# Second-layer weight preparation moved within the image cycle, in larger pieces and in place, and the S1 product split seven to two

## The chip, the cores and the metric

The kernel runs on one core of one Trainium2 chip. The metric is the device time of one execution in microseconds, as the median of several runs. A profiled execution is recorded beside them, with the instructions of each engine: PE (TensorE matmul) with its weight loads (PEld), DVE (VectorE), ACT (ScalarE), POOL (GpSimd) and SP (SyncE, which only issues DMAs here).

## What is computed

Sixteen images of 256 channels, 28 by 28, pass through a group norm, two "table lookup" convolutions with batch norm, a squeeze-and-excite gate and residual additions, in float32. Each 3x3 convolution is done per channel c by a soft choice among 16 centroids of the 9-element patch:

```python
d = jnp.sum(p * p, axis=-1)[..., None] - 2.0 * jnp.einsum('bncs,cks->bnck', p, centroids) + jnp.sum(centroids * centroids, axis=-1)[None, None]
attn = jax.nn.softmax(-d, axis=-1)
lut = jnp.einsum('cks,cso->cko', centroids, w_sub)
out = jnp.einsum('bnck,cko->bno', attn, lut)
...
out = amm_conv3x3(out1, centroids1, wsub1)
out = relu(bn_inference(out, ...1))
out = amm_conv3x3(out, centroids2, wsub2)
out = bn_inference(out, ...2)
out = se_layer(out, se_w1, se_b1, se_w2, se_b2)
return x + relu(out + gn(x))
```

The kernel multiplies the softmax weights with the centroids first (logits, exponentials, numerators "na" for taps 0 to 7, "nb" for tap 8 and the denominators), divides, and multiplies the resulting 9 stacks "q" of 128 rows by w_sub.

## The kernel before

All 16 images go through layer 1, then all through layer 2. An image is four blocks, (channel half hh, row half t) in the order of BLOCKS, and a block is two steps; so an image takes eight steps, n*8 to n*8 + 7, and the products of an image trail its logits by five to twelve steps. Nothing is scheduled by a tool: `at(step, sub, function, ...)` puts a job into a list, and the list, sorted by step and then by the fraction `sub`, is the order in which each engine gets its instructions. Each engine takes its own in order. Below, the remainder of a step is its number modulo 8.

In every step PE does 16 logit matmuls (sub 0.1), the denominators "nb" or the numerators "na" of an earlier block (1.0), 16 more logit matmuls (1.1) and one product of 9 stacks (2.0). ACT takes the exponentials of the logits out of PSUM; DVE takes reciprocals, spreads them (`spread`) and scales the numerators into the q buffers (`scale_a`); POOL scales what ACT copied (`scale_q`, 1.3).

The products use seven multiplications in place of eight (L43): A11, S1, S3, S2, S4, A12, A22, with the q buffers of two blocks subtracted from each other on POOL (`mix`, L523) between them. Product S1 is cut in two: KO[:8], eight stacks, in step 6 of an image, and KO[8:], one stack, in step 7. KO puts the pairs of stacks in the order 2 to 7, 8, 0, 1, and POOL makes the mixed buffers in the same order, pair (0, 1) last, at (step 5, 2.5). PSUM is a ring of four double banks with a fixed role per step.

Patch tiles `pt` are two, each loaded by six DMAs of SP at sub 1.5, two steps before the logits that read them. The loads wait until the second logits of their own step have released the tile. The patches come from DRAM copies home1 (layer 1) and home2 (layer 2). In layer 1, POOL scatters an image's result, channel-sorted by a rank found in the first images, from hpad into home2 with four indirect DMAs (`to_home2`, L590) at remainders 4 to 6: both halves of channel block 0, then those of block 1. The next image's group norm, its home1 write (`to_home1`, remainder 4) and the load of the image after (remainder 6) stand in the same list.

While layer 1 runs, the tables of layer 2 are made from the unsorted weights. This preparation is what the change moves:

- h0: image 0's result, kept in DRAM until the rank is known, is loaded and scattered (`h0_load`, `h0_put`).
- codes: centroids2 in two layouts, scattered by rank into d_sk and d_ks.
- sub: wsub2, in three pieces per channel half (4 and 4 stacks and 1), scattered into d_wa and d_wb.
- wd: the distance table, gathered from d_sk with nine DMAs (`prep_wd0`), spread on DVE (`prep_wd1`), squared on POOL and centred with three matmuls (`prep_wd2`, `prep_wd3`), centred by its mean and stored to d_wd[1] (`prep_wd4`).
- cw: the numerator tables, gathered from d_ks with eight DMAs, made on DVE (cwa) and POOL (cwb, four parts), stored to d_cwa and d_cwb.
- sums: the combined weights S1 to S4, two stacks at a time: four loads, four POOL additions or subtractions, four stores.

All of it goes through one staging tile of 128 x 1568 (`stage`, tag "pb", one buffer), so each load waits until the tile's former readers, stores and scatters included, are done. In layer 2 the same buffer holds the wide path's z.

Of the kernel before, what the change touches and what calls it, by code (L numbers as in the profile page):

```python
# [43 lines left out]
    (5, "A11", 0, KO), (6, "S1", 0, KO[:8]), (7, "S1", 0, KO[8:]), (8, "S3", 1, KO), (9, "S2", 0, KO),  # L44
# [29 lines left out]
def kernel(  # L74
# [628 lines left out]
    def sub_load(o, part):  # L703
        n = 4 * C if part < 2 else C
        nc.sync.dma_start(stage()[:, :n], wsub2[o * P : (o + 1) * P, part * 4 * C : part * 4 * C + n])

    def sub_put(o, part):
        n = 4 * C if part < 2 else C
        scatter(d_wa if part < 2 else d_wb, 2 + part, o, pw["st"][:, :n])

    def prep_wd0():
        st = stage()
        nc.gpsimd.memset(st[:, :512], 0.0)
# [21 lines left out]
    def prep_wd4():  # L735
        st = pw.pop("st")
# [3 lines left out]
        nc.sync.dma_start(d_wd[1], st[:, 512:1536])  # L740
# [17 lines left out]
    def prep_cwb(part):  # L758
# [7 lines left out]
        if part == 3:  # L766
            pw.pop("st")
            nc.sync.dma_start(d_cwb, st[:, 512:1536])

    def sums_load(k0):  # L770
        st = stage()
        n = min(2, NS - k0)
        for hh in range(2):
            for o in range(2):
                at0 = 256 * (2 * hh + o)
                if n == 2:
                    nc.sync.dma_start(
                        st[:, at0 : at0 + 256].rearrange("p (s n) -> p s n", n=P),
                        view(d_wa, (hh * 8 + k0) * P * C + o * P, [[C, P], [P * C, 2], [1, P]]),
                    )  # L780
                else:
                    nc.sync.dma_start(st[:, at0 : at0 + P], d_wb[hh * P : hh * P + P, o * P : (o + 1) * P])

    def sums_put(k0):
        st = pw.pop("st")
        n = min(2, NS - k0)
        f = {w: st[:, 256 * i : 256 * i + P * n] for i, w in enumerate(("A11", "A21", "A12", "A22", "S1"))}
        for dst, a, b, op in (
            ("S1", "A21", "A22", ALU.add), ("A21", "A11", "A21", ALU.subtract),
            ("A22", "S1", "A11", ALU.subtract), ("A12", "A12", "A22", ALU.subtract),  # L790
        ):
            nc.gpsimd.tensor_tensor(f[dst], f[a], f[b], op)
        for n0, w in (("S1", "S1"), ("S3", "A21"), ("S2", "A22"), ("S4", "A12")):
            nc.sync.dma_start(d_ws[n0][:, k0 : k0 + n, :], f[w].rearrange("p (s n) -> p s n", n=P))
# [256 lines left out]
    at(49, 0.6, prep_wd0)  # L1051
    at(50, 0.3, prep_wd1)
    for part in range(3):
        at(51 + 2 * part, 0.02, prep_wd2, part)
        at(51 + 2 * part, 2.1, prep_wd3, part, 51 + 2 * part)
    at(59, 1.9, prep_wd4)
    at(60, 0.6, prep_cw0)
    at(61, 1.9, prep_cwa)
    for part in range(4):
        at((67, 68, 75, 76)[part], 2.3, prep_cwb, part)  # L1060
    at(92, 2.3, load_se)
    for n in range(5):
        at(82 + 8 * n, 0.6, sums_load, 2 * n)
# [198 lines left out]
```

## Time and profile before

| | us |
|---|---|
| median of 3 runs | 2680.17 |
| lowest and highest run | 2678.79, 2683.46 |
| profiled execution | 2684.49 |
| its span, first to last instruction | 2683.0 |
| PE busy in it | 2613.8 |
| longest stretches off PE in the chain of waits | 244.01 to 260.51, 492.00 to 507.90 |

The mean granted clock of PE over the span is 0.993. The page lists busy times of each engine; the chain of waits follows the work that ended last back from the end, and lists its pieces by start and length; the windows view sums each engine's busy time between chosen bounds. In the trace every fp32 matmul shows as two records, and one stack of a product takes 0.65 us on PE. An image is best measured from the start of one of its products to the same product of the next image; in the prediction that is the product at remainder 0. Step 24 starts its product at 282.68, step 128 at 1348.24, and step 16 at 190.39.

### The profile page before, as it was taken

What the parts mean: (1) busy time and instruction counts of PE and PEld (TensorE: products, weight loads), DVE (VectorE), ACT (ScalarE), POOL (GpSimd) and SP (SyncE); (2) the same over time, 40 slices, a digit from 0 to 9 for tenths busy, and PEclk for the clock granted to TensorE, in tenths of its full rate; (3) what the DMA queues carried; (4) which work ended last, traced back from release to release, by engine and by line L of the source; (5) the groups of instructions that cost most, each with busy time, mean ns of one, the idle gap of its engine ahead of it and who ended that gap; (6) DMA issues with size and microseconds to landing.
All of it is one profiled execution on the core that took longest, in us unless ns stands there. A gap on an engine that the chain in (4) does not pass through costs nothing.

```text
span 2683.0 us, 85705 instructions
## 1 busy us (share of the span) xinstructions
PE 2613.8 (97%) x36984; PEld 1261.1 (47%) x36984; DVE 1773.8 (66%) x3786; ACT 1354.7 (50%) x1873; POOL 1903.7 (71%) x1334
## 2 busy tenths in 40 slices
PE   4999999999999999999999999999999999999997
PEld 1344444444444444444444444444444444444444
DVE  4785666667666556656577767677767677767675
ACT  2443444444445444444455555555555655555653
POOL 3755677666776666766578687788787788787786
PEclk8999999999999999999999999999999999999999
DMA  8665667755666666666584555545555555555551
GB/s 180 162 158 147 155 159 201 195 139 138 158 165 168 178 156 145 164 176 158 127 191 108 111 127 123 116 111 109 122 127 123 116 113 108 121 127 123 116 114 51
DMA packets 223337, 374.39 MB, mean 140 GB/s; under 512 B 30360, under 2 KB 193736, under 8 KB 222952
## 3 DMA queue, kind: packets, MB, share of 16 engines
q1 hardware_dynamic: 216008, 334.87, 54.0%
q0 software_dynamic: 6944, 33.95, 3.5%
q8 instruction: 295, 4.83, 0.8%
q14 instruction: 90, 0.74, 0.1%
HBM read 288.93 MB, written 79.80 MB: 137 GB/s over the span
## 4 chain that ended last, share of the span: by engine, by line
PE 86%; DMA 1%; POOL 1%; issue 1%; DVE 1%; ACT 0%; SPq 0%; POOLq 0%; DVEq 0%; ACTq 0%
PE acc L518 46%; PE lg L384 15%; PE na L434 12%; PE nb L448 12%; DMA home<-hpad,col 1%; POOL qp L527 1%; PE sep L814 0%; ACT e L395 0%; DMA pt<-home 0%; PE sep L803 0%; DVE qp L510 0%; DVE rb L491 0%; POOL home L590 0%; POOL qo L525 0%; PE sqp L288 0%
## 5 line engine op out<-in xcount | busy, mean ns | idle before, releaser
L395 ACT ACTIVATE e<-lg 128x784 f32<-128x784 f32 x960 | 738.8, 821 | 720.2 <-PE lg L384 714.9
L527 POOL TENSOR_TENSOR qp<-qp,qp 128x784 f32<-128x784 f32 x512 | 944.6, 1870 | 163.5 <-DVE qp L510 163.0
L518 PE MATMUL acc<-qp,w_S 128*128 128x392 f32 x2048 | 743.2, 503 | 7.7 <-POOL qp L527 6.3
L491 DVE STREAM_SHUFFLE rb<-r 128x392 f32<-128x392 f32 x1024 | 550.6, 604 | 0.0
L518 PE MATMUL acc<-qp,w_A 128*128 128x392 f32 x1536 | 546.5, 499 | 0.1
L518 PEld LDWEIGHTS acc<-qp,w_S 128*128 128x128 f32 x2048 | 376.1, 190 | 356.6 <-POOL qp L527 39.1
L384 PE MATMUL lg<-pt,wd 32*32 32x392 f32 x16384 | 500.6, 504 | 27.0 <-DMA pt<-home 16.3
L518 PEld LDWEIGHTS acc<-qp,w_A 128*128 128x128 f32 x1536 | 284.1, 190 | 247.9 <-DVE qp L510 37.6
L510 DVE TENSOR_TENSOR qp<-na,rb 128x784 f32<-128x784 f32 x352 | 334.1, 972 | 98.1 <-PE na L434 84.9
L462 DVE SCALAR_TENSOR_TENSOR r<-nb,kst,r 128x392 f32<-128x392 f32 x128 | 79.9, 624 | 464.5 <-ACT r L458 464.5
L448 PE MATMUL nb<-e,cwb 64*32 64x392 f32 x8192 | 382.4, 497 | 2.1 <-issue 1.0
L434 PE MATMUL na<-e,cwa 64*32 64x392 f32 x8192 | 377.5, 494 | 0.1
L476 DVE RECIPROCAL r<-r 128x392 f32<-128x392 f32 x128 | 333.2, 2603 | 4.4
L499 POOL TENSOR_TENSOR qp<-qp,rb 128x784 f32<-128x784 f32 x160 | 297.4, 1871 | 2.4
L448 PEld LDWEIGHTS nb<-e,cwb 64*32 64x32 f32 x8192 | 181.4, 107 | 195.8 <-issue 57.1
L384 PEld LDWEIGHTS lg<-pt,wd 32*32 32x32 f32 x16384 | 127.5, 103 | 309.0 <-issue 261.6
L499 POOL TENSOR_TENSOR qo<-qo,rb 128x392 f32<-128x392 f32 x128 | 132.0, 1031 | 197.7 <-DVE rb L487 197.5
L434 PEld LDWEIGHTS na<-e,cwa 64*32 64x32 f32 x8192 | 182.5, 106 | 186.8 <-issue 78.0
L590 POOL DMA_INDIRECT home<-hpad,col x60 | 60.6, 1011 | 185.9 <-DMA home<-hpad,col 91.2
L458 ACT ACTIVATE r<-nb,kst 128x392 f32<-128x392 f32 x128 | 86.8, 678 | 177.4 <-PE nb L448 177.4
L419 POOL TENSOR_TENSOR z<-z,mx 128x1568 f32<-128x1568 f32 x32 | 92.1, 2879 | 86.4 <-DVE mx L413 86.4
L504 ACT COPY qp<-na 128x784 f32<-128x784 f32 x160 | 130.1, 813 | 26.0 <-PE na L434 24.0
(154 smaller groups left out, 1744.5 us busy)
## 6 DMA issues: line engine op xcount, KB each, us to landing
pt<-home SPq DMA_DIRECT2D x768, 209.0 KB
pt<-home SPq DMA_DIRECT2D x756, 104.5 KB
home<-xpad SPq DMA_DIRECT2D x31, 899.0 KB
xt<-in_x SPq DMA_DIRECT2D x30, 784.0 KB
out_dram<-y SPq DMA_DIRECT2D x32, 392.0 KB
w_S<-d_wS SPq DMA_DIRECT2D x4, 576.0 KB
st<-in_wsub SPq DMA_DIRECT2D x4, 512.0 KB
st<-d_wa SPq DMA_DIRECT2D x16, 128.0 KB
```

The costliest lines, as they stand in the source:

```text
L384: nc.tensor.matmul(bk[32 * c : 32 * c + 32, :N].rearrange("p (r w) -> p r w", w=W), lhsT=wts["wd", u["hh"]][32 * i : 32 * i + 32, mm, c, : ...
L395: nc.scalar.activation(eg[:, 2 * i : 2 * i + 2, :], bk[:, :, :N], AF.Exp, scale=2.0)
L419: nc.gpsimd.tensor_tensor(zk, zk, mx.unsqueeze(2).to_broadcast([P, N // 4, K]), ALU.subtract)
L434: nc.tensor.matmul(bs[32 * i : 32 * i + 32, r, :N], lhsT=wts["cwa", u["hh"]][64 * r : 64 * r + 64, mm, i, :], rhs=es[64 * r : 64 * r + 64, ...
L448: nc.tensor.matmul(bs[32 * i : 32 * i + 32, r, :N], lhsT=wts["cwb", u["hh"]][64 * r : 64 * r + 64, mm, i, :], rhs=es[64 * r : 64 * r + 64, ...
L476: nc.vector.reciprocal(u["r"], u["r"])
L491: nc.vector.stream_shuffle(rb[:, r, :], u["r"], mask_of(2 * mm + r))
L499: nc.gpsimd.tensor_tensor(q, q, u.pop(("rb", mm)), ALU.mult)
L504: nc.scalar.copy(pair(u, mm), u.pop(("na", mm))[:, :, :N])
L510: nc.vector.tensor_mul(pair(u, mm), u.pop(("na", mm))[:, :, :N], rb)
L518: nc.tensor.matmul(accs[key][:, :N], lhsT=wl[w][:, k, :], rhs=us["q", k], start=first and n == 0, stop=last and n == len(ks) - 1,)
L527: nc.gpsimd.tensor_tensor(pair(out_u, mm), pair(in0, mm), pair(in1, mm), ALU.subtract)
```

## The change

The steps and sub-positions of most preparation jobs are changed. wsub2 is loaded in two pieces per channel half in place of three (the ninth stack comes with the second). The clearing of the wd staging tile, the stores of wd and cwb, and the arithmetic and the stores of the sums become jobs of their own (`prep_clear`, `prep_keep`, `sums_make`, `sums_put`). The sums are made three stacks at a time, and S1 and S2 are written over A22 and A11, so that four tiles suffice in place of five. Product S1 is cut 7 to 2.

```diff
-    (5, "A11", 0, KO), (6, "S1", 0, KO[:8]), (7, "S1", 0, KO[8:]), (8, "S3", 1, KO), (9, "S2", 0, KO),
+    (5, "A11", 0, KO), (6, "S1", 0, KO[:7]), (7, "S1", 0, KO[7:]), (8, "S3", 1, KO), (9, "S2", 0, KO),
...
     def sub_load(o, part):
-        n = 4 * C if part < 2 else C
+        n = (4 + part) * C
         nc.sync.dma_start(stage()[:, :n], wsub2[o * P : (o + 1) * P, part * 4 * C : part * 4 * C + n])
     def sub_put(o, part):
-        n = 4 * C if part < 2 else C
-        scatter(d_wa if part < 2 else d_wb, 2 + part, o, pw["st"][:, :n])
+        scatter(d_wa, 2 + part, o, pw["st"][:, : 4 * C])
+        if part == 1:
+            scatter(d_wb, 4, o, pw["st"][:, 4 * C : 5 * C])
+    def prep_clear():
+        nc.gpsimd.memset(stage()[:, :512], 0.0)
     def prep_wd0():
-        st = stage()
-        nc.gpsimd.memset(st[:, :512], 0.0)
+        st = pw["st"]
...
     def prep_wd4():
-        st = pw.pop("st")
+        st = pw["st"]
...
-        nc.sync.dma_start(d_wd[1], st[:, 512:1536])
+    def prep_keep(dst):
+        nc.sync.dma_start(dst, pw.pop("st")[:, 512:1536])
...
-        if part == 3:
-            pw.pop("st")
-            nc.sync.dma_start(d_cwb, st[:, 512:1536])
+    def sums_of():
+        return {w: pw["st"][:, 3 * P * i : 3 * P * i + 3 * P] for i, w in enumerate(("A11", "A21", "A12", "A22"))}
     def sums_load(k0):
...
+        n = min(3, NS - 1 - k0)
+        for w, t in sums_of().items():
+            hh, o = {"A11": (0, 0), "A21": (0, 1), "A12": (1, 0), "A22": (1, 1)}[w]
+            nc.sync.dma_start(
+                t[:, : n * P].rearrange("p (s n) -> p s n", n=P),
+                view(d_wa, (hh * 8 + k0) * P * C + o * P, [[C, P], [P * C, n], [1, P]]),
+            )
+            if n < 3:
+                nc.sync.dma_start(t[:, n * P :], d_wb[hh * P : hh * P + P, o * P : (o + 1) * P])
+    def sums_make():
+        f = sums_of()
         for dst, a, b, op in (
-            ("S1", "A21", "A22", ALU.add), ("A21", "A11", "A21", ALU.subtract),
-            ("A22", "S1", "A11", ALU.subtract), ("A12", "A12", "A22", ALU.subtract),
+            ("A22", "A21", "A22", ALU.add), ("A21", "A11", "A21", ALU.subtract),
+            ("A11", "A22", "A11", ALU.subtract), ("A12", "A12", "A11", ALU.subtract),
         ):
             nc.gpsimd.tensor_tensor(f[dst], f[a], f[b], op)
+    def sums_put(k0):
+        f = sums_of()
+        pw.pop("st")
+        for n0, w in (("S1", "A22"), ("S3", "A21"), ("S2", "A11"), ("S4", "A12")):
+            nc.sync.dma_start(d_ws[n0][:, k0 : k0 + 3, :], f[w].rearrange("p (s n) -> p s n", n=P))
...
-        at(20 + 3 * o, 0.6, h0_load, o)
+        at(24 + 2 * o, 0.6 + 2 * o, h0_load, o)
         for r in range(2):
-            at(*(((21, 1.77), (22, 2.95)), ((24, 2.95), (25, 1.78)))[o][r], h0_put, o, r)
-        at(32 + 2 * o, 0.6, codes_load, o)
+            at(25 + 2 * o + r, 0.2 if r else 1.9, h0_put, o, r)
+        at(32 + 2 * o, 2.6, codes_load, o)
         for i in range(2):
-            at(33 + 2 * o, 1.78 if o == i == 0 else 1.805, codes_put, o, i)
-        for part in range(3):
-            c = 36 + 6 * o + 2 * part
-            at(c, 0.6, sub_load, o, part)
-            at(c + 1, (1.77, 2.7, 1.78, 1.805)[(3 * o + part) % 4 if o == 0 else (3, 0, 1)[part]], sub_put, o, part)
-    at(49, 0.6, prep_wd0)
-    at(50, 0.3, prep_wd1)
+            at(33 + 2 * o, 1.9, codes_put, o, i)
+        for part in range(2):
+            c = 40 + 8 * o + 2 * part
+            at(c, 2.6, sub_load, o, part)
+            at(c + 1, 1.9, sub_put, o, part)
+    at(56, 1.95, prep_clear)
+    at(57, 1.6, prep_wd0)
+    at(60, 0.3, prep_wd1)
     for part in range(3):
-        at(51 + 2 * part, 0.02, prep_wd2, part)
-        at(51 + 2 * part, 2.1, prep_wd3, part, 51 + 2 * part)
-    at(59, 1.9, prep_wd4)
-    at(60, 0.6, prep_cw0)
-    at(61, 1.9, prep_cwa)
+        c = (65, 67, 73)[part]
+        at(c, 0.02, prep_wd2, part)
+        at(c, 2.1, prep_wd3, part, c)
+    at(75, 1.9, prep_wd4)
+    at(75, 2.7, prep_keep, d_wd[1])
+    at(80, 2.6, prep_cw0)
+    at(83, 1.9, prep_cwa)
     for part in range(4):
-        at((67, 68, 75, 76)[part], 2.3, prep_cwb, part)
+        at((83, 84, 89, 91)[part], (2.3, 0.9, 1.9, 1.9)[part], prep_cwb, part)
+    at(91, 2.7, prep_keep, d_cwb)
     at(92, 2.3, load_se)
-    for n in range(5):
-        at(82 + 8 * n, 0.6, sums_load, 2 * n)
-        at(83 + 8 * n, 2.3, sums_put, 2 * n)
+    for n in range(3):
+        at(96 + 8 * n, 2.6, sums_load, 3 * n)
+        at(97 + 8 * n, 1.9, sums_make)
+        at(98 + 8 * n, 2.6, sums_put, 3 * n)
```

More of the change, by code (lines that the diff above doesn't have):

```diff
@@ L765, in prep_cwb @@
             nc.gpsimd.tensor_add(f[:, m], f[:, m], ones_b[:, m % 4, :].unsqueeze(1).to_broadcast([P, 4, 32]))
-        if part == 3:
-            pw.pop("st")
-            nc.sync.dma_start(d_cwb, st[:, 512:1536])
+    def sums_of():
+        return {w: pw["st"][:, 3 * P * i : 3 * P * i + 3 * P] for i, w in enumerate(("A11", "A21", "A12", "A22"))}
     def sums_load(k0):
[L771 to L787, printed above, removed]
+        stage()
+        n = min(3, NS - 1 - k0)
[7 more added lines that the diff above has]
+                nc.sync.dma_start(t[:, n * P :], d_wb[hh * P : hh * P + P, o * P : (o + 1) * P])
```

2 lines of the change are left out of this document (removed).

## The prediction

> **What bounds the kernel now.** I read the page first, then the chain of waits in order of time, and then the windows view, cut at the first product of an image. One row of the page says who sets the time:
>
> ```profile
> PE 2613.8 (97%) x36984; PEld 1261.1 (47%) x36984; DVE 1773.8 (66%) x3786; ACT 1354.7 (50%) x1873; POOL 1903.7 (71%) x1334
> ```
>
> The work of PE itself is not changed, so only stretches in which PE waits, or runs slowly around a wait, can be won. The windows view gives their size (columns: bounds, length, busy time of PE, PEld, DVE, ACT, POOL, granted clock, DMA share, GB/s):
>
> ```profile
> 190.39:239.25 48.86, 46.56 (x589) 22.83 (x589) 30.06 (x72) 17.72 (x24) 35.32 (x36) 0.97 0.45 95
> 239.25:282.68 43.43, 40.95 (x569) 18.28 (x567) 25.42 (x59) 20.04 (x28) 25.18 (x25) 0.96 0.78 218
> 282.68:614.37 331.69, 326.92 (x4623) 157.89 (x4623) 208.25 (x482) 152.05 (x208) 224.01 (x170) 1.00 0.66 169
> 614.37:859.33 244.96, 243.33 (x3464) 117.80 (x3463) 159.67 (x364) 114.23 (x156) 166.90 (x140) 1.00 0.63 157
> 859.33:1187.82 328.49, 326.26 (x4618) 158.60 (x4617) 204.09 (x477) 152.20 (x208) 220.95 (x171) 1.00 0.65 164
> 1187.82:1230.91 43.09, 43.09 (x590) 21.75 (x589) 25.58 (x62) 17.62 (x24) 28.89 (x25) 1.00 0.49 103
> 1230.91:1268.10 37.19, 37.19 (x568) 17.85 (x567) 23.17 (x53) 20.41 (x28) 22.39 (x16) 1.00 0.74 200
> 1348.24:1430.01 81.77, 80.91 (x1152) 38.31 (x1151) 56.53 (x112) 40.88 (x54) 59.58 (x39) 1.00 0.76 179
> 2314.30:2394.71 80.41, 80.41 (x1158) 39.02 (x1157) 56.71 (x113) 46.68 (x66) 63.02 (x39) 1.00 0.53 118
> ```
>
> Rows six and seven are one image of layer 1 with next to no preparation: 43.09 + 37.19 = 80.28 us. An image of layer 2 takes 80.41 with PE busy throughout, so there is nothing to win in layer 2 behind its first image. Against 80.28 an image, steps 24 to 56 lose 331.69 - 321.12 = 10.57, steps 56 to 80 lose 4.12, steps 80 to 112 lose 7.37: 22.06 us. Image 2 loses 48.86 - 43.09 = 5.77 in its first half and 43.43 - 37.19 = 6.24 in its second. The first image of layer 2 loses 81.77 - 80.41 = 1.36. This is the pot.
>
> The chain shows where the loss starts:
>
> ```profile
> 244.01 8.51 issue
> 252.53 7.98 DMA home<-hpad,col
> ...
> 445.80 6.12 PE acc L518 x18
> 456.51 6.12 PE acc L518 x18
> 467.34 6.12 PE acc L518 x18
> 478.06 6.12 PE acc L518 x18
> 492.00 7.94 DMA home<-hpad,col
> 500.20 7.70 DMA home<-hpad,col
> 529.03 6.12 PE acc L518 x18
> ```
>
> It leaves PE at the scatter of an image into home2, in steps with remainder 4 to 6. POOL issues the second half of a channel block only when the first has landed, and ScalarE's next accumulator copy into hpad waits until the scatter has read hpad; behind it stand the exponentials, and behind POOL's scatter the mixes that feed product 6. The four products of steps 40 to 43 stand 10.71, 10.83 and 10.72 us apart although pieces of wsub2 are scattered in steps 41 and 43; the piece put in step 45 meets the scatter, and step 46 stalls.
>
> **Part 1: where the pieces stand.** One ordinary image by steps (remainders 2 to 7, 0, 1), same columns:
>
> ```profile
> 1205.58:1216.29 10.71, 10.71 (x157) 5.30 (x146) 7.19 (x17) 4.32 (x6) 10.15 (x7) 1.00 0.48 105
> 1216.29:1227.12 10.83, 10.83 (x159) 5.58 (x148) 5.97 (x15) 5.08 (x7) 3.30 (x4) 1.00 0.44 90
> 1227.12:1237.83 10.71, 10.71 (x157) 5.29 (x146) 6.38 (x15) 6.78 (x9) 3.82 (x8) 1.00 0.60 144
> 1237.83:1248.54 10.71, 10.71 (x158) 5.19 (x146) 5.26 (x12) 4.93 (x7) 4.86 (x5) 1.00 0.90 296
> 1248.54:1258.75 10.21, 10.21 (x157) 5.38 (x144) 6.34 (x16) 4.81 (x7) 9.24 (x6) 1.00 0.67 164
> 1258.75:1264.29 5.54, 5.54 (x143) 2.31 (x130) 4.56 (x10) 3.88 (x5) 3.40 (x2) 1.00 0.38 114
> 1264.29:1275.00 10.71, 10.71 (x154) 4.96 (x146) 7.08 (x17) 4.33 (x6) 10.71 (x8) 1.00 0.81 169
> 1275.00:1285.73 10.73, 10.73 (x160) 5.19 (x146) 5.99 (x14) 3.88 (x5) 8.16 (x7) 1.00 0.46 96
> ```
>
> The DMA engines are 0.90 busy at remainder 5 and at 0.44 to 0.48 at remainders 1 to 3. The old list put loads and puts at every remainder; the new one issues loads behind the patches of remainders 0 and 2, and POOL's part at the end of remainders 1 and 3. The bytes stay the same. SyncE's own waits say what else goes (steps 32 to 115):
>
> ```profile
> SPq L705 <- DMA d_wa<-st,col: 30.7, 4, 9.0
> SPq L794 <- POOL st L792: 24.8, 13, 5.0
> SPq L768 <- POOL st L765: 9.8, 1, 9.8
> ```
>
> SyncE stood before the patch loads because a load at 0.6 wanted the staging buffer that the scatter just issued was still reading, or because stores were issued right behind POOL's arithmetic. Now most of a step lies between.
>
> Steps 24 to 56 lose 10.57. The steps of remainders 0 to 3 that held pieces lost nothing (the four products above). Bounds: all 10.57 gained, or nothing, if the bytes cost wherever they lie. Nearest are those four products, so I leave 0.4 us an image for the 640 KB scatters of steps 43 and 51, which run into remainder 4: gain 10.57 - 1.6 = 9.0.
>
> Image 2: the second half (6.24) has the h0 load of step 20 and the scatters of 21 and 22 among its own; all of them go to steps 24 to 28. I leave 1.0: gain 5.2 (bounds 0 and 6.24). The 5.77 of the first half belong to the ranking, which does not move.
>
> Steps 56 to 80 take over the three centring matmuls. One of them in its old place:
>
> ```profile
> 569.13 0.88 PE L288 MATMUL sqp<-sq,nhalf_sb 128*128 128x384 f32 x2 [0.34 <-DVE nrm L340]
> ```
>
> All three now stand right behind a group-norm matmul that has the same PSUM slot (steps 65, 67, 73), so each waits for DVE's two short reads, as this one did. 0.34 + 0.88 is 1.2 each, 3.6 with queueing 3.9 (bounds 2.2 without a wait, 5 with one of 0.8); another 0.5 for the centring and its store in step 75. 4.4 against 4.12: loss 0.3.
>
> **Part 2: larger pieces in place.** Four POOL subtractions or additions for three stacks, three times, in place of five times four for two:
>
> ```profile
> L792 POOL TENSOR_TENSOR st<-st x20: 455/730/739, 899.7 to 1229.7; 128x256 f32<-128x256 f32 x16, 128x128 f32<-128x128 f32 x4
> ```
>
> 128 columns take 0.455, 256 take 0.730, so 384 take an estimated 1.005, four 4.0 us. They are put at the end of remainder 1, ahead of POOL's additions into hpad:
>
> ```profile
> 1281.19 1.85 POOL L499 TENSOR_TENSOR qp<-qp,rb 128x784 f32<-128x784 f32 x1
> 1285.62 2.01 POOL L562 TENSOR_TENSOR hpad<-hpad,half_sum 128x392 f32<-128x392 f32 x2 [2.57 <-DVE hpad L555]
> ```
>
> The gap is 2.57, so the additions come 1.4 us later; their readers are DVE's addition at the end of the next step and product 12 two steps on. Nothing, unless the load (768 KB, behind the patches) is late too: then POOL holds four instructions and the mixes behind them, with the same two steps of slack. What is not covered is part 0 of the cwb table: it overwrites the half of the staging buffer that the cwa store, issued in the same step 83, still reads. If that store takes the 7.70 us of the scatter above, POOL stands about 3 us, and the home2 scatter of step 84 comes late by what passes this cover (step 68 of the old order):
>
> ```profile
> 737.20 0.29 POOL L763 COPY st<-kst 128x128 f32<-128x128 f32 x1
> ...
> 742.91 1.09 POOL L590 DMA_INDIRECT home<-hpad,col  x1 [3.13 <-ACT hpad L569]
> ```
>
> Two parts of 2.6 us follow each other there instead of one, so up to 3 us lost, or none if the store lands in 4; I take 1.0. With 0.7 for the last two cwb parts and their store, 0.6 for load_se (unmoved) and 0.3 for the sums, steps 80 to 112 lose 2.6 in place of 7.37: gain 4.8.
>
> Against the larger pieces speaks the Trainium skill, "DMA: Bandwidth & Descriptors", section "Queues, rings and completion order": each DMA engine takes the descriptors of one issuing queue in order, so patch loads queue behind a 768 KB piece. No row here shows the order itself; 786 KB at the 296 GB/s of the fullest step are 2.7 us. By the rule the next patches land that much later; they are issued two steps before their logits, so the sum would stay, and only with the engines full does it lead to the third rival.
>
> **Part 3: product S1, seven stacks and two.** PE's work per image is equal; two matmuls (0.65 us) go from step 6 to step 7. It takes POOL's last mix off the first product. The old stall at that place:
>
> ```profile
> 517.97 0.93 PE L518 MATMUL acc<-qp,w_S 128*128 128x392 f32 x2 [0.56 <-POOL qp L527]
> ```
>
> Where POOL is late anyway (first image, first image of layer 2) it saves about 0.6 each: 1.2. In the 30 other images it must cost nothing. PE's numerators of step 7, and with them DVE's scaling, now come 0.65 earlier, while the reciprocal that feeds the scaling still hangs on the denominators of step 6; DVE has this idle time before it:
>
> ```profile
> 2305.96 0.97 DVE L510 TENSOR_TENSOR qp<-na,rb 128x784 f32<-128x784 f32 x1 [0.85 <-PE na L434]
> ```
>
> **Sum.** 9.0 + 5.2 - 0.3 + 4.8 + 1.2 = 19.9 us. The profiled execution took 2684.49 (span 2683.0): 2664.6. It lies 4.3 above the median of the runs, 2680.17, so 2660.3.
>
> **Rivals.**
> 1. Half the gain (2668 to 2674). If the loss in steps 80 to 112 comes of the full DMA engines at remainder 5 (0.90) and not of POOL and SyncE, the 4.8 stays, and so does half of steps 24 to 56: 19.9 - 4.8 - 4.5 = 10.6, 2669.6. For it: SyncE's 24.8 us there delay loads that have two steps of slack. Against: the stores leave remainders 3 and 4.
> 2. It does not do what it says (2675 to 2682): as many bytes and POOL microseconds, stalls only change places; what stays is 1.2, so 2679. For it: the DMA share of a losing image (0.63 to 0.66) is hardly above the 0.61 of a clean one (0.49 and 0.74 by halves), so no room was lacking on average. Against: the four products. The same time follows if the split binds on DVE: 32 x 0.65 = 20.8 would eat all; the idle 0.85 speaks against.
> 3. Slower: the 640 KB scatters and 768 KB stores begun in remainder 3 lengthen the home2 scatter of 4 and 5 in every one of the twelve images 3 to 14, as in the image of 445.80 to 529.03 us, which lost 83.23 - 80.28 = 2.95. 12 x 2.95 = 35.4 in place of 22.06, less 5.2 and 1.2: +6.9, 2687. It decides from a mean loss of 2.8 us an image. Against: pieces of 512 KB at those places cost nothing in steps 41 and 43.
>
> **How the numbers follow.** Forecast (gain over 12) 0.66, rival 1 0.14, rival 2 0.11, rival 3 0.09. The best case is all 22.06 + 6.24 + 2 less the bare matmuls, 1.8: 2651.7. The range 2651 to 2674 holds the first two, 0.80. About 0.2% is what a measurement can tell: faster than 2674.8 0.80, within 0.11, slower 0.09.
>
> **What would show it.** Right: images between steps 24 and 120 within 0.5 us of 80.28 but for 65 to 75; SyncE's three waits gone; no POOL wait of PE in step 46; layer 2 still 80.41. Wrong: an image of layer 2 above 80.5 (split), a home2 scatter after step 83 later than 7 us into its step (cwb), stalls at remainder 5 that stay (rival 1), or a second half-scatter waiting over 7 us in most images (rival 3).

## The result and the profile after

| | median us | lowest to highest | runs |
|---|---|---|---|
| kernel before, beside these runs | 2678.96 | 2675.07 to 2683.46 | 7 |
| kernel after | 2665.16 | 2659.91 to 2672.14 | 7 |

The ratio is 0.9948, with a 95% interval of 0.9935 to 0.9961: the change makes the kernel 0.5% faster. The profiled execution after took 2666.47 us (span 2665.0), 18.0 less than the one before. The windows of the kernel after, cut at the same products as in the prediction (columns as there):

```profile
188.47:233.38 44.91, 43.22 (x600) 21.75 (x589) 29.41 (x71) 17.61 (x24) 34.81 (x36) 1.00 0.43 91
233.38:278.29 44.91, 40.74 (x577) 19.16 (x567) 25.40 (x59) 20.09 (x28) 23.69 (x23) 0.92 0.70 184
278.29:601.71 323.42, 321.78 (x4627) 157.45 (x4616) 203.90 (x476) 151.94 (x208) 222.55 (x168) 1.00 0.71 178
601.71:848.18 246.47, 243.44 (x3474) 119.13 (x3469) 159.09 (x366) 113.73 (x156) 161.22 (x120) 1.00 0.63 153
848.18:1173.25 325.07, 322.13 (x4628) 158.50 (x4617) 205.52 (x478) 151.74 (x208) 223.78 (x185) 1.00 0.68 165
1333.71:1413.50 79.79, 79.79 (x1161) 38.74 (x1151) 56.49 (x112) 40.87 (x54) 59.58 (x39) 1.00 0.76 183
2377.05:2457.36 80.31, 80.31 (x1167) 39.27 (x1156) 56.74 (x113) 46.65 (x65) 63.06 (x39) 1.00 0.53 118
```

| stretch | predicted change | profiled change |
|---|---|---|
| image 2, first half (steps 16 to 20) | 0 | 48.86 to 44.91: -3.95 |
| image 2, second half (20 to 24) | -5.2 | 43.43 to 44.91: +1.48 |
| steps 24 to 56 | -9.0 | 331.69 to 323.42: -8.27 |
| steps 56 to 80 | +0.3 | 244.96 to 246.47: +1.51 |
| steps 80 to 112 | -4.8 | 328.49 to 325.07: -3.42 |
| first image of layer 2 | -0.6 | 81.77 to 79.79: -1.98 |
| each further image of layer 2 | 0 | 80.41 to 80.31: -0.10 |

Three entries stand out. The second half of image 2 did not gain. Every image of layer 2 gained 0.10, where nothing was to be won. And steps 80 to 112 still lose over 3 us, most of them at one place, which the list of POOL's instructions shows (steps 83 and 84):

```profile
890.88 0.29 POOL L768 COPY st<-kst 128x128 f32<-128x128 f32 x1 [2.21 <-DMA d_cwa<-st]
896.13 1.09 POOL L590 DMA_INDIRECT home<-hpad,col  x1 [0.17 <-ACT xpad L349]
905.14 0.97 POOL L590 DMA_INDIRECT home<-hpad,col  x1 [7.91 <-DMA home<-hpad,col]
```

The first row is the wait that the prediction named, the first part of cwb behind the cwa store, 2.21 us; the second is the home2 scatter behind it, 8.59 us into its step in place of 6.90 in nearly every other image. Step 86 then lasts 13.69 us, 9.40 in a clean image.

Below, a step starts with its first numerators or denominators matmul; images are named by the steps in which they lie.

### The profile page after: what moved, and what is told of

It reads as the page before. It is cut to its first block, busy times and chain, and to the rows that moved or that the text cites. A ratio compares the mean times of both kernels' runs of the same rounds, so it can differ in the third digit from the quotient of the medians.

```text
span 2665.0 us, 85694 instructions
## 1 busy us (share of the span) xinstructions
PE 2596.2 (97%) x36984; PEld 1266.4 (48%) x36984; DVE 1768.7 (66%) x3786; ACT 1353.4 (51%) x1873; POOL 1902.5 (71%) x1326
## 4 chain that ended last, share of the span: by engine, by line
PE 86%; DMA 2%; POOL 1%; issue 1%; ACT 0%; DVE 0%; POOLq 0%; ACTq 0%; DVEq 0%
PE acc L518 46%; PE lg L384 15%; PE na L434 12%; PE nb L448 12%; DMA home<-hpad,col 2%; POOL qp L527 1%; PE sep L819 0%; ACT e L395 0%; PE sep L808 0%; POOL home L590 0%; PE sqp L288 0%; DVE y L860 0%; DVE y L863 0%; ACT xpad L349 0%; ACT hpad L569 0%
## 5 line engine op out<-in xcount | busy, mean ns | idle before, releaser
L384 PE MATMUL lg<-pt,wd 32*32 32x392 f32 x16384 | 489.9, 503 | 26.6 <-DMA pt<-home 16.6
L448 PEld LDWEIGHTS nb<-e,cwb 64*32 64x32 f32 x8192 | 191.9, 107 | 178.0 <-issue 36.7
L384 PEld LDWEIGHTS lg<-pt,wd 32*32 32x32 f32 x16384 | 121.8, 103 | 306.7 <-issue 253.4
```

The costliest lines, as they stand in the source:

```text
L384: nc.tensor.matmul(bk[32 * c : 32 * c + 32, :N].rearrange("p (r w) -> p r w", w=W), lhsT=wts["wd", u["hh"]][32 * i : 32 * i + 32, mm, c, : ...
L448: nc.tensor.matmul(bs[32 * i : 32 * i + 32, r, :N], lhsT=wts["cwb", u["hh"]][64 * r : 64 * r + 64, mm, i, :], rhs=es[64 * r : 64 * r + 64, ...
```

## The experiments

The runs were made on several chips, on which the kernel before took medians of 2672 to 2681 us. So ratios are compared, or runs of one call, which share a chip.

### The split alone, and the placement alone

The kernel before with one line changed:

```diff
-    (5, "A11", 0, KO), (6, "S1", 0, KO[:8]), (7, "S1", 0, KO[8:]), (8, "S3", 1, KO), (9, "S2", 0, KO),
+    (5, "A11", 0, KO), (6, "S1", 0, KO[:7]), (7, "S1", 0, KO[7:]), (8, "S3", 1, KO), (9, "S2", 0, KO),
```

> The kernel before with product S1 split seven and two, nothing else. Theory A, formed from the two traces: besides the first images of both layers (0.8 and 2.0 us) the split gains 0.10 us in every image, because in the old step 7 only two matmuls of the product stand between two groups of logits and the second group waits for ScalarE's exponentials (0.97 in place of 0.87 us); so about 30 x 0.10 + 2.8 = 5.8 us, a clean image of layer 2 at 80.31 instead of 80.41. Rival B, as predicted: it matters only where POOL is late, 1.2 us in all, and a clean image stays at 80.41.

Measured: 2661.66 against 2672.49, ratio 0.9960 (0.9944 to 0.9976). An image of layer 2 takes 80.31, 80.41 in the kernel before. Both theories are too small: 10.8 us, where A expected 5.8 and B 1.2 (the interval is 6.4 to 15.0 us). The 0.10 us an image of A is there. The opposite kernel has that line undone in the kernel after.

> The kernel after with product S1 split eight and one again: the new placement, pieces and sums without the new split. Theory A, formed after the run of the split alone: the split lets the second half-scatter into home2 land 0.8 us later before PE stands (20.5 in place of 19.7 us after the start of the step with remainder 4), and the placement by itself gains next to nothing; so without it the images of layer 1 lose 0.5 to 0.8 us each wherever that half lands after 19.7, every image loses 0.10, the first image of layer 2 loses 2: 10 to 13 us slower than the kernel after, ratio to the kernel before 0.998 to 1.002. Rival B, the prediction's sum: the placement brings 18.7 of the 19.9 us and the split 1.2, so 0.993 to 0.996 remains.

Measured: 2684.70 against 2681.28, ratio 1.0012 (0.9999 to 1.0025). Theory A holds in the time: placement, larger pieces and sums in place bring nothing that can be measured by themselves.

The kernel before was run once more on that chip, for a second profile:

> The kernel before once more, unchanged, for a second profiled execution. Theory A: the stalls of PE in steps 96, 104 and 111 (1.6, 2.2 and 2.3 us), at whose start no other engine releases PE and which follow a late packet of PE's own instructions by 1 to 2 us, move or shrink from one execution to the next, while the stalls on POOL and ScalarE behind the scatter (images 4, 7 and 9 and the first image of layer 2) return within 0.5 us. Rival B: they belong to the sums of steps 82 to 115 and return at the same places with the same lengths.

Measured: 2683.21 in its one run. The windows of the three kernels for steps 24 to 56, 56 to 80 and 80 to 112, first the kernel before again, then the placement alone, then (on another chip) the split alone:

```profile
282.13:613.13 331.00, 326.46 (x4626) 158.32 (x4623) 208.76 (x482) 152.29 (x208) 224.23 (x171) 1.00 0.66 170
613.13:858.81 245.68, 244.00 (x3467) 117.39 (x3462) 159.62 (x364) 114.32 (x156) 166.46 (x139) 1.00 0.63 157
858.81:1187.94 329.13, 327.73 (x4622) 158.91 (x4617) 204.36 (x477) 152.18 (x208) 222.54 (x171) 0.99 0.66 164
```

```profile
281.08:605.96 324.88, 324.44 (x4621) 158.25 (x4617) 204.29 (x477) 152.13 (x208) 222.32 (x168) 1.00 0.70 178
605.96:859.32 253.36, 247.38 (x3475) 118.92 (x3469) 159.41 (x365) 114.04 (x156) 161.32 (x120) 1.00 0.60 148
859.32:1189.98 330.66, 325.72 (x4621) 157.38 (x4617) 206.74 (x481) 151.90 (x208) 225.84 (x186) 1.00 0.66 164
```

```profile
275.12:602.08 326.96, 324.35 (x4634) 158.01 (x4623) 208.65 (x482) 152.17 (x208) 223.79 (x170) 1.00 0.68 172
602.08:846.28 244.20, 242.60 (x3467) 117.93 (x3463) 159.24 (x363) 114.28 (x156) 167.31 (x140) 1.00 0.63 158
846.28:1168.02 321.74, 321.10 (x4626) 157.23 (x4616) 203.95 (x478) 152.05 (x208) 220.40 (x170) 1.00 0.66 168
```

So the placement wins 6.1 us in steps 24 to 56, where the pieces of wsub2 moved, gives back 7.7 in steps 56 to 80, where the preparation of the distances now stands, and 1.5 in steps 80 to 112. Of the 7.7, the three centring matmuls are 3.6, step 78 behind the scatter of step 76 is 2.3, and stalls that no engine ends, in steps 56 and 71, are 3.8; some smaller stalls of before went.

The split alone can't be set against these rows, since its chip was faster with the kernel before too (2672.49 against 2681.28). On the chip of the placement alone, the kernel after with its sums stored later (a run below) took 326.60, 248.06 and 326.80: there the split lost 1.7 in the first stretch and won 5.3 and 3.9 in the others. On the chip of the split alone, the kernel after with one store later (also below) took 321.58, 246.27 and 325.12: with the split too the placement won 5.4 and gave back 2.1 and 3.4. All these are single profiles.

What the split does shows in the list of PE's instructions. In the kernel before, step 46 has four waits inside product S1, one for each pair that POOL mixes:

```profile
511.56 1.58 PE L518 MATMUL acc<-qp,w_S 128*128 128x392 f32 x4 [0.66 <-POOL qp L527]
513.36 1.58 PE L518 MATMUL acc<-qp,w_S 128*128 128x392 f32 x4 [0.21 <-POOL qp L527]
515.17 1.58 PE L518 MATMUL acc<-qp,w_S 128*128 128x392 f32 x4 [0.22 <-POOL qp L527]
...
517.97 0.93 PE L518 MATMUL acc<-qp,w_S 128*128 128x392 f32 x2 [0.56 <-POOL qp L527]
```

The last of them, for the fourth pair, is gone in the kernel after, since both stacks of that pair belong to step 7; here its step 38:

```profile
423.72 1.58 PE L518 MATMUL acc<-qp,w_S 128*128 128x392 f32 x4 [0.45 <-POOL qp L527]
425.51 1.58 PE L518 MATMUL acc<-qp,w_S 128*128 128x392 f32 x4 [0.21 <-POOL qp L527]
427.31 0.93 PE L518 MATMUL acc<-qp,w_S 128*128 128x392 f32 x2 [0.22 <-POOL qp L527]
```

POOL's mixes stand behind the scatters into home2, so their start is set by the landing of the second half-scatter of the first channel block. That landing, counted from the start of the step with remainder 4, and what the step with remainder 6 lasts over its shortest length (10.06 with eight and one, 9.40 with seven and two), from the lists of POOL's and PE's instructions:

| kernel | step | landing | excess | landing less excess |
|---|---|---|---|---|
| before | 46 | 22.82 | 3.11 | 19.7 |
| before again | 70 | 21.17 | 1.55 | 19.6 |
| placement alone | 78 | 23.06 | 3.35 | 19.7 |
| placement alone | 86 | 24.32 | 4.62 | 19.7 |
| after | 38 | 21.99 | 1.48 | 20.5 |
| after | 78 | 22.95 | 2.47 | 20.5 |
| after | 86 | 24.82 | 4.29 | 20.5 |

These are steps in which PE does wait for POOL. The last column is the time by which the scatter must have landed: 19.6 to 19.7 with the old split, 20.5 with the new. In the kernel before, the twelve scatters of steps 28 to 117 landed at 17.6 to 22.8, eight of them past the bound. But PE did not wait for POOL in all eight. The waits view of PE from 185 to 1210 us (steps 16 to 114) has these rows for POOL's mixes (us in all, times, longest), first the kernel before, then the split alone:

```profile
PE acc L518 <- POOL qp L527: 3.7, 6, 1.5
```

```profile
PE acc L518 <- POOL qp L527: 1.9, 3, 1.5
```

The longest of each stands in step 22. The others of the kernel before stand in steps 46 and 78 (there POOL came late from a part of the cwb table), and in its second profile in 46, 70 and 78. In steps 38, 86, 94, 102 and 110, whose scatters landed past the bound too, product S1 takes its shortest time, 5.46 us; what these steps last longer, 0.1 to 0.9 us, lies inside the denominators' matmuls ahead of it, and no engine ends it. An estimate from this: up to 0.8 us in each of steps 46, 70 and 78, 2.4 us; with 3.0 for 0.10 us in 30 images, 0.8 for the first image and 0.6 to 2.0 for the first image of layer 2 (80.39 and 81.77 in the two profiles of the kernel before, 79.8 with the split) that is 6.8 to 8.2 us. It lies within the interval of the measurement, but some 3 us of the 10.8 have no cause that a trace shows.

The 0.10 us in every image has another cause. Step 7 in layer 2, before and after:

```profile
1584.91 0.93 PE L518 MATMUL acc<-qp,w_S 128*128 128x392 f32 x2
1585.76 1.04 PE L384 MATMUL lg<-pt,wd 32*32 32x392 f32 x32
```

```profile
1567.81 1.58 PE L518 MATMUL acc<-qp,w_S 128*128 128x392 f32 x4
1569.33 0.94 PE L384 MATMUL lg<-pt,wd 32*32 32x392 f32 x32
```

Between two groups of logits stood only two matmuls of the product; the second group was slowed (1.04), which four matmuls remove (0.94). That ScalarE's exponentials, which free the PSUM of the first group, are what it met is argued from the order, not shown by a wait.

As to the second profile of the kernel before: step 111 lost 2.4 (2.3 in the first), step 104 0.7 (1.3), step 96 0.1 (1.1), and step 112 1.5 that it had not lost. The placement alone, whose sums are made and stored in other steps, loses 1.2, 0.9 and 2.2 in 96, 104 and 111. So they are not tied to the sums of the old steps, and theory B falls. A holds in part: of the three stalls one stayed, and the stalls behind the scatter moved too, by up to 1.4 (step 134, 11.88 and 10.50), more than the 0.5 it allowed. Step 111 in the first profile of the kernel before, and the DMA queues in 1169.3 to 1180.7 and in 1180.7 to 1182.0:

```profile
1180.75 1.00 PE L384 MATMUL lg<-pt,wd 32*32 32x392 f32 x22
1183.23 0.87 PE L384 MATMUL lg<-pt,wd 32*32 32x392 f32 x10 [1.48 <-issue]
```

```profile
q1 hardware_dynamic: 909, 1.76, 70.7%
q0 software_dynamic: 48, 0.29, 6.2%
```

```profile
q0 software_dynamic: 30, 0.16, 31.7%
q1 hardware_dynamic: 58, 0.09, 24.8%
q8 instruction: 1, 0.02, 4.9%
```

For 11.4 us no packet of the instruction queue q8 came, and the next one is followed by a stall that no engine ends. That PE had run out of instructions is the likeliest reading, but it was not tried by itself. The split alone has one such stall left in steps 96 to 112, of 1.5 us in 111; whether the split or its chip thinned them out stays open.

### The steps that lost: the store of step 75, the tables of step 83, the centring

```diff
-    at(75, 2.7, prep_keep, d_wd[1])
+    at(78, 2.6, prep_keep, d_wd[1])
```

> The kernel after with the store of the second layer's centred distance table (d_wd[1]) moved from the end of step 75 to the end of step 78. Theory A: an image loses what the landing of the second half-scatter into home2 passes 10.0 us of the step with remainder 5, and this store takes DMA bandwidth from it; without it the halves of step 76 land by 3.2 and 9.7 us of step 77 (4.75 and 12.2 before), step 78 goes from 11.87 to 9.4 us, the image from 82.50 to 80.1: 2.4 us faster. Rival B: the centring on POOL and VectorE in step 75 is what makes POOL late, and it stays: image 82.2 to 82.6, no gain.

Measured: 2661.71, ratio 0.9957 (0.9943 to 0.9971), within 0.1 us of the split alone on the same chip. The image of steps 74 to 81 took 82.58: no gain, theory A falls for this store. Nor is it the centring (B): the scatter was issued on time, at 6.90 us of step 76, and then its halves took 8.4 and 7.7 us (the second landed at 824.21):

```profile
808.11 1.07 POOL L590 DMA_INDIRECT home<-hpad,col  x1 [3.79 <-ACT hpad L569]
816.48 0.97 POOL L590 DMA_INDIRECT home<-hpad,col  x1 [7.30 <-DMA home<-hpad,col]
```

The first half of this image takes 8.0 to 8.9 us in all eleven profiles whose home1 stores were not moved, the kernel before among them, for a reason that stays open. The second half differs. With the old preparation (here the split alone) it was issued at 820.30 and landed at 824.97, in 4.67 us, and SyncE's queue there shows why:

```profile
812.61 1.37 SPq L361 DMA_DIRECT2D home<-xpad  x2
823.87 0.35 SPq L768 DMA_DIRECT2D d_cwb<-st  x1
824.31 0.60 SPq L368 DMA_DIRECT2D pt<-home  x1
```

Waiting for POOL with the cwb store, SyncE issued the next patches at 824.31, when the second half had nearly landed; in the kernel after they go out before the second half is issued (820.51), which then takes 7.49:

```profile
819.76 0.59 SPq L368 DMA_DIRECT2D pt<-home  x1
```

By these rows the wait on L768 of 9.8 us, which the prediction counted among the losses, had kept the patches out of the scatter's way; no run moved the patches alone.

```diff
-    at(83, 1.9, prep_cwa)
+    at(81, 1.9, prep_cwa)
```

> The kernel after with the numerators' table cwa made in step 81 in place of 83, so that its store has landed when POOL starts the first part of cwb in step 83. Theory A: POOL's wait of 2.21 us for that store makes the first half-scatter of step 84 1.7 us late, and this alone makes step 86 last 13.69 us; without it the scatter is issued at 6.9 us of step 84 and step 86 lasts 9.4 to 9.7: 4.0 to 4.3 us faster. Rival B: two parts of cwb one behind the other, 5.2 us of POOL, are too much ahead of the scatter even without the wait: it stays 1 us or more late, step 86 still lasts over 11 us, gain under 2.5. If the load of the table has not landed by the end of step 81, VectorE stands there instead, and the image loses in step 82.

Measured: 2659.01, ratio 0.9945 (0.9927 to 0.9964), 2.7 us below the run before it on the same chip, which the intervals alone can't tell apart. In the profile, step 86 lasts 9.40 (13.95 there) and its image 80.42 (84.58); an "issue" stall in step 96 takes 0.9 back in the next. Theory A, by POOL's list:

```profile
885.62 0.29 POOL L768 COPY st<-kst 128x128 f32<-128x128 f32 x1
891.34 1.09 POOL L590 DMA_INDIRECT home<-hpad,col  x1 [0.62 <-ACT hpad L569]
```

The parts still stand one behind the other, but end before hpad is ready: the wait for the store was all of it.

```diff
-        c = (65, 67, 73)[part]
+        c = (66, 72, 74)[part]
```

> The kernel after with the three centring matmuls in steps 66, 72 and 74, which have no group-norm matmul, in place of 65, 67 and 73, which have one with the same PSUM slot. Theory A: the wait for VectorE's reads of that slot goes (0.3 to 0.5 us each) and the bare 0.88 stays: steps 65, 67, 73 each 1.1 to 1.3 shorter, 66, 72, 74 each 0.88 longer, about 1 us faster. Rival B: the matmul costs the same 1.2 wherever it stands: no change.

Measured: 2660.61, ratio 0.9954 (0.9938 to 0.9969); steps 66, 72 and 74 lasted 1.24 to 1.38 longer than the 10.71 of such steps, as 65, 67 and 73 had lasted 1.1 to 1.3 longer. B holds in its number, by another wait:

```profile
709.41 1.88 PE L434 MATMUL na<-e,cwa 64*32 64x392 f32 x40 [0.66 <-DVE st L289]
```

In an even step the numerators behind it need the PSUM slot that VectorE is still reading.

### Do the places matter?

Two kernels put pieces at remainders from which the change had taken them.

```diff
-            c = 40 + 8 * o + 2 * part
+            c = 44 + 8 * o + 2 * part
```

> The kernel after with the four large pieces of wsub2 shifted by four steps: loads in steps 44, 46, 52 and 54, puts in 45, 47, 53 and 55, that is at the remainders that the change avoids. Theory A: where the pieces stand matters for them: the put of 512 KB at the end of step 45 (and 53) and the load of 640 KB in 46 meet the second channel block's scatter and POOL's mixes, and the images of steps 42 to 49 and 50 to 57 lose 2 us or more each (80.1 becomes 82 or more). Rival B: with the new split the place is covered too, and each loses under 0.6.

```diff
-        at(98 + 8 * n, 2.6, sums_put, 3 * n)
+        at(99 + 8 * n, 2.6, sums_put, 3 * n)
```

> The kernel after with the stores of the three pieces of the sums issued at the end of steps 99, 107 and 115 in place of 98, 106 and 114, so that 768 KB run into the step of the home2 scatter. Theory A: the scatter's halves share the DMA engines with them and land 1 to 3 us later (20.0 to 20.6 us after the start of the step with remainder 4 becomes 21 to 23), the steps 102, 110 and 118 grow by 0.5 to 2.5 us: 2 to 6 us slower in all, images 12 to 14. Rival B: the engines have room, the halves land within 0.5 us of where they did, and nothing is lost.

Measured, one run each on the chip of the placement alone (kernel before 2681.28): 2681.05 and 2674.47. With the shifted pieces the images of steps 42 to 49 and 50 to 57 took 83.17 and 84.07; in the other kernel, where these pieces stand as in the kernel after, 81.35 and 82.61: 1.8 and 1.5 lost, less than A and more than B. The second half of the scatter took 7.8 and 8.3 us there, 5.9 and 6.6 in the other. POOL's next scatter, in step 46, ends a wait that the profile puts down to the load of a piece, though the half-scatter had landed only 0.7 us before:

```profile
506.67 1.01 POOL L590 DMA_INDIRECT home<-hpad,col  x1 [4.19 <-DMA st<-in_wsub]
```

Behind it POOL issues the piece's own scatter, and the mixes begin 1.3 us later than they would without it, so not all of the loss comes through the DMA engines.

The late stores cost nothing: the halves of the scatter of step 100 took 7.0 and 5.7 us (7.0 and 6.5 in the kernel after), and steps 102, 110 and 118 lasted 9.55, 9.40 and 9.40. So A falls for them, and with it the third rival's price for stores of 768 KB.

### The scatter's neighbours: the home1 stores

```diff
-                        at(g + 5 - (b > 0), 1.92, to_home1, b + 1, q)
+                        at(g + 5, 1.92, to_home1, b + 1, q)
```

> The kernel after with the two stores of the next image's padded map into home1 (899 KB each) issued one step later, at the end of the step with remainder 5 in place of 4, so that the first half-scatter into home2 no longer shares the DMA engines with them. Theory A, the landing of the second half decides: the first half takes 4 to 5 us in place of 6.9, the second half lands 1.5 us or more earlier, steps 22, 78 and 86 shrink by 1 to 3 us each: 3 to 7 us faster than the kernel after (ratio to the kernel before 0.992 to 0.994). Rival B: the stores meet the second half or the next image's patches instead, and the sum of the two halves stays within 0.5 us: no gain, or a loss in the steps of remainder 0 where the late patches are read.

Measured: 2680.24 against 2673.56, ratio 1.0018 (1.0004 to 1.0032). From step 22 to 126 every step with remainder 6 takes 9.40, step 22 itself among them (17.38 in the kernel after); but PE now waits for patches that wait for home1, 9 times:

```profile
PE lg L384 <- DMA pt<-home: 19.1, 9, 4.9
```

Both theories are right in part. That the landing decides is shown; B named the price. The issue of the two halves in steps 100 and 101 in POOL's list, and then the DMA queues while the second was under way (1074.9 to 1078.1):

```profile
1068.23 1.07 POOL L590 DMA_INDIRECT home<-hpad,col  x1 [5.78 <-ACT hpad L569]
1074.85 0.97 POOL L590 DMA_INDIRECT home<-hpad,col  x1 [5.55 <-DMA home<-hpad,col]
```

```profile
q0 software_dynamic: 80, 0.46, 38.7%
q1 hardware_dynamic: 60, 0.10, 14.0%
```

The same window of the kernel after (1066.4 to 1072.8):

```profile
q1 hardware_dynamic: 598, 1.39, 67.8%
q0 software_dynamic: 80, 0.46, 23.0%
```

The same 80 packets of 0.46 MB take 3.3 us beside 0.10 MB of other traffic and 6.4 beside 1.39 MB. The Trainium skill, "DMA: Bandwidth & Descriptors", section "Queues, rings and completion order", says that a DMA engine takes turns between the queues that have work, a packet of each; these two rows agree with it.

The opposite: variance, application and stores of the group norm one step earlier.

```diff
-                    at(g + 4 - (b > 0), 2.1, gn_var, b + 1, step=g + 4 - (b > 0))
+                    at(g + 4 - 2 * (b > 0), 2.1, gn_var, b + 1, step=g + 4 - 2 * (b > 0))
...
-                        at(g + 5 - (b > 0), 1.9, gn_apply, b + 1, q)
-                        at(g + 5 - (b > 0), 1.92, to_home1, b + 1, q)
+                        at(g + 5 - 2 * (b > 0), 1.9, gn_apply, b + 1, q)
+                        at(g + 5 - 2 * (b > 0), 1.92, to_home1, b + 1, q)
```

> The kernel after with the next image's group-norm variance, its application and the two home1 stores (899 KB each) one step earlier, at remainders 2 and 3 in place of 3 and 4, so that the stores are through before the home2 scatter starts and long before the patches that read them. Theory A, formed after the run with the stores later, in which every step of remainder 6 took 9.40 us and the loss stood where patches waited for home1: here neither is late, the two halves together take 10 to 12 us in place of 13.5 to 18.8, steps 22, 78 and 86 fall to 9.4 (or within 0.5), images 2, 9 and 10 gain about 6, 2.4 and 4.2 us: 10 to 14 us faster than the kernel after, ratio to the kernel before 0.989 to 0.992. Rival B: the engines are short of room at remainder 3 too (pieces, patches), the halves shrink by under 1 us or the patches of remainder 4 come late, and the gain stays under 3 us.

Measured: 2669.43 against 2680.07, ratio 0.9963 (0.9949 to 0.9978). The mechanism of A holds: steps 22, 78 and 86 last 9.40, 9.92 and 9.54. But the matmul of the variance now stands in an even step, and a wait that neither theory had eats the gain:

```profile
PE na L434 <- DVE gn_var L338: 10.1, 13, 0.8
```

### Six and three, and the home1 stores half a step earlier

```diff
-    (5, "A11", 0, KO), (6, "S1", 0, KO[:7]), (7, "S1", 0, KO[7:]), (8, "S3", 1, KO), (9, "S2", 0, KO),
+    (5, "A11", 0, KO), (6, "S1", 0, KO[:6]), (7, "S1", 0, KO[6:]), (8, "S3", 1, KO), (9, "S2", 0, KO),
```

> The kernel after with product S1 split six and three in place of seven and two. Theory A: what the split covers is POOL's last and fourth pair of mixes, which the two stacks moved to step 7 read; the stack moved now hangs on a short mix of 1.0 us that PE does not wait for, so nothing more is gained: within 1.5 us of the kernel after, clean images at 80.31 in layer 2 as before. Rival B: each matmul moved to step 7 lets the scatter land 0.33 us later, the stalls of steps 22, 78 and 86 shrink by 0.3 each, and no other is left: about 2 us faster. If VectorE's scaling of the numerators, which stand another 0.33 us earlier, binds, every image of layer 2 grows above 80.4.

Measured: 2659.55 against 2673.56, ratio 0.9940 (0.9919 to 0.9961), not to be told from the kernel after. Step 78 lasts 2.50 over its shortest length with a landing at 22.98, so the bound stays at 20.5, as A has it, and most images of layer 2 stay at 80.31 to 80.41.

```diff
-                        at(g + 5 - (b > 0), 1.9, gn_apply, b + 1, q)
-                        at(g + 5 - (b > 0), 1.92, to_home1, b + 1, q)
+                        at(*((g + 4, (0.5, 1.1)[q]) if b else (5, 1.9)), gn_apply, b + 1, q)
+                        at(*((g + 4, (0.52, 1.12)[q]) if b else (5, 1.92)), to_home1, b + 1, q)
...
-    at(83, 1.9, prep_cwa)
+    at(81, 1.9, prep_cwa)
```

> The kernel after with two edits: cwa made in step 81 (as in the run of that edit alone), and the group norm's application and the home1 stores of the next image moved from the end of the step with remainder 4 to its first half, one channel block ahead of and one behind the copy of the denominators on ScalarE; the group-norm matmul stays where it was, so PE gets no new wait on VectorE (0.85 us an image in the run with everything one step earlier). Theory A: the stores start 3 to 5 us earlier, in the part of the step in which the DMA engines are a quarter busy, the two halves of the scatter take 10 to 12 us, every step of remainder 6 takes 9.4 to 9.6 us, image 2 gains 5 to 6, image 9 2, image 10 4.2: 11 to 13 us faster than the kernel after, ratio to the kernel before 0.989 to 0.991. Rival B: ScalarE's 1 us ahead of the denominators' copy makes the reciprocal late and every image of layer 1 loses 0.3 to 1 us in step 3 or 5, or the first half-scatter still shares its time with the stores; then the gain is that of the cwa edit alone, ratio 0.993 to 0.995.

Measured: 2661.93 against 2680.10, ratio 0.9926 (0.9910 to 0.9942). It is surely faster than the kernel before, and by its ratio 0.2% faster than the kernel after, though the two intervals overlap a little. The second half of image 2 and steps 80 to 112:

```profile
236.60:274.90 38.30, 38.19 (x579) 17.78 (x567) 25.43 (x59) 19.40 (x27) 23.77 (x23) 1.00 0.81 215
846.65:1167.74 321.09, 321.09 (x4628) 160.23 (x4617) 205.18 (x476) 151.63 (x208) 223.69 (x185) 1.00 0.69 167
```

44.91 and 325.07 in the kernel after. The two halves together take 10.6 to 12.9 us in twelve of the thirteen images; those of step 76 still take 15.2, and step 78 lasts 12.70. So the mechanism of theory A holds but for that image, and the ratio lies between the two theories.

## Why the prediction came out as it did, point by point

- **The total** was met (13.8 us of gain, 19.9 forecast), but not by the steps that made it up. 18.7 us were put down to the places of the pieces and 1.2 to the split. Alone, the split gives 10.8 us and the places lose 3.4, within what can be measured of nothing (each of these figures is uncertain by 3 to 4 us). That the total fell into the range is largely luck.
- **The step that failed is Part 3**: "Where POOL is late anyway (first image, first image of layer 2) it saves about 0.6 each". Its mechanism was right, POOL's last mix leaves the first product, and a stall of exactly that kind was quoted from step 46. The mistake was to hold POOL late in two images only. In the two profiles of the kernel before, PE waits for it in steps 46 and 78 and, once, 70 of layer 1 as well. The 0.10 us in every image had not been seen at all.
- **Part 1, steps 24 to 56**: 9.0 forecast, 8.27 found, 6.1 without the split. That pieces cost less at remainders 0 to 3 is shown by the shifted ones (1.5 to 1.8 us an image, in one run, and part of it is POOL's own time).
- **Image 2, second half**: "all of them go to steps 24 to 28", gain 5.2. The pieces went and the stall stayed, 14 to 17 us for step 22 with them or without. It is the home1 stores, whose move brings the step to 9.40. The profile of before had shown it in the chain, a scatter of 7.98 us; the prediction looked for what stood beside it among the pieces only. The 3.95 us that the first half gained come from steps 17 and 19; on one chip step 19 kept its excess with the split and without, so what they hang on stays open.
- **Steps 56 to 80**: a loss of 0.3 forecast, 1.51 found, 7.7 without the split. The three centring matmuls took 3.6 us (3.9 forecast). Of the rest that the placement lost alone, 2.3 us came through the scatter of step 76, which SyncE's old wait had covered, as far as the rows above tell, and 3.8 are stalls that no engine ends. "SyncE's three waits gone" was right, and that it is all gain was not. One of its terms was wrong from the start: the matmuls without a wait are 3 x 0.88 = 2.6 by the row that it shows, not the 2.2 of its bound or the 1.8 of its best case, which moves the lower end of the range by 0.8.
- **Steps 80 to 112**: 4.8 forecast, 3.42 found. The wait of cwb for the cwa store was named and given 1.0 of a range up to 3; it measured 4.3, since both parts, the scatter and its second half are late by it. And the loss of before that this gain was drawn from was not that of the sums alone: stalls in steps 96, 104 and 111 stand there with the sums in other steps too.
- **The rivals**: the third decides from scatters lengthened by the larger pieces; the late 768 KB stores lengthened none. The second, that the placement only changes the places of the stalls, is what the placement by itself does; that the split binds on VectorE did not come about.
- **Its own signs**: layer 2 at 80.31 and step 46 without a wait on POOL were as said. But the sign against it for cwb came, a home2 scatter 8.59 us into step 84, and beside the steps that it had excepted three images lay over 80.8: 81.50 us from step 32, 81.41 from step 48 and 84.32 from step 80.

## What to carry to other kernels

When a stall ends on one engine in many iterations by a little, ask what bound it lies at before costing the edit next to it: a small edit that moves the bound, here one mix taken off a product, is worth up to its margin in every iteration that passes it. Count the waits themselves, too: eight transfers passed the bound here, and the waiting engine stood for it in two or three. A change with several parts can come out near its predicted sum with most of the terms wrong; the parts one by one (two kernels here) tell that at once. And a wait on a queue that feeds prefetches can be what keeps a critical transfer's neighbours away: before counting its removal as a gain, look at what will then be issued earlier, and beside what.

## What the hardware showed beside

- A half-scatter of 0.46 MB took 3.3 us with little beside it, 6 to 7 us beside home1 stores and patches, and 8.0 to 8.9 us for one image, in every kernel that had the stores there.
- Instructions come by DMA in packets of 16 KB, 295 of them on queue q8, some 9.4 us apart; that these are PE's is taken from the stalls behind late ones. In layer 1 some were 11 to 14 us apart, with PE standing 1 to 2 us behind several of these without any other engine ending the wait. The Trainium skill, "Runtime: NRT & Kernel Launch", section "Instruction fetch mechanics", has fetches in blocks of 16 KiB over a DMA queue and calls their cost mostly hidden; the packets agree with the first part. These stalls speak against the second where the DMA engines are full, but their cause is only read from the times.
- PE ran slower for some microseconds after the long wait of step 22: the granted clock of the stretch with it was 0.92 in the kernel after (0.5 for 6.8 us from 259.0 on), and 1.00 in the two kernels with earlier home1 stores, where step 22 lasted 9.40 and 10.23.
